# Channel mixing cut into six stages with a fixed turn on TensorE

## The chip, the cores and the metric

The kernel runs on one core of one Trainium2 chip. A core has five engines that each work through their own instructions in order and wait for one another by semaphores: TensorE (PE in the profile), VectorE (DVE), ScalarE (ACT), GpSimd (POOL) and SyncE (SP), which here issues every DMA. The metric is the time of one execution on the device in microseconds, the median over several executions.

## The reference

The input is x of 8 batches x 256 tokens x 512 channels, and a context of the same shape. Two blocks follow each other. The first is a transformer block: self-attention, cross-attention to the context, and an MLP of 512 to 2048 to 512, each with a layernorm ahead of it. The second is a recurrent block: time mixing (a scan over the tokens with a decaying state) and then channel mixing. The change lies in channel mixing, with the output of time mixing (`out`, `g`) and the residual `x`:

```python
og = normalised(out) * gn_w + gn_b
x1 = x + og * g @ Wo.T
xc = _ln(x1, ln2_w, ln2_b)
sx2 = jnp.concatenate([state[:, 0:1] - xc[:, :1], xc[:, :-1] - xc[:, 1:]], axis=1)
xk2 = xc + sx2 * ffn_maa_k
xr2 = xc + sx2 * ffn_maa_r
rr = jax.nn.sigmoid(xr2 @ Wfr.T)
kk = jnp.square(jax.nn.relu(xk2 @ Wfk.T))
return x1 + rr * (kk @ Wfv.T)
```

So there are four products of 256 x 512 by 512 x 512 for each batch: with Wo, Wfr, Wfk and Wfv.

## The kernel before

**Tiling.** A batch of 256 tokens is two tiles of 128 tokens (t = 0, 1), and the 512 channels are four chunks of 128 (KC). A product takes operands with the channels on partitions, so normalised rows are first transposed on TensorE (`to_t`, L217: eight 128 x 128 transposes for a batch, in two groups of four, one bank of PSUM each). Every operand of a product is split into a high and a low part in the fp32r type, and `mm3` (L185 to L187) adds three matmuls: high by high, high by low, low by high. `proj_n` gives tokens on partitions (24 matmuls of 512 columns for a batch, 12 for each token tile); `proj_t` gives channels on partitions (48 matmuls of 256 columns).

**Stages.** The whole program is straight code for 8 batches: self-attention, cross-attention, two halves of the MLP, then time mixing and channel mixing. Time mixing has stages a, b, e, c, d: a to e make its projections, c is the scan within blocks of 16 tokens and lies on GpSimd (L713 to L755) with sums on VectorE (L715, L730, L743, L762), d carries the state over the blocks: small transposes (L780, and L217 into the tile wtp), an update with 128 matmuls (L807), a scan on VectorE (L824), 128 output matmuls (L834), sums into on_ (L837) and a store of the normalised result to `yg` (L847). In the profile each L807 and L834 of the program shows as two matmuls.

d loads its first rows, dd, into a staging tile (L777). The two staging tiles (pool `wst`) go round between d's rows, the rows of v that ScalarE copies for c (L702, L703) and others; L703 writes into tiles that the c before it reads in L755.

**Channel mixing** has two stages for each batch, `front` (f) and `back` (g). f loads yg and g (L875, L877), transposes yg, scales and gates it (L883, L897), splits it (L890, L891), loads the residual x4 (L901, which the profile shows at the helper's line L288), multiplies by Wo and adds x4 (L902), normalises (`layernorm`, L194 to L205, with two small operations on GpSimd, L197 and L198), transposes again and makes xr and xk (`mixes`, L909 to L916, split by L890 and L891). g multiplies xr by Wfr and takes a tanh (L924), multiplies xk by Wfk and takes relu squared (L930, L931), split into kk (L932, L933), multiplies that by Wfv, gates, adds to x4 (L938, L939) and stores (L942).

**What sets the order.** `SEQ` lists the stages in the order in which they are written; each gets a priority from its batch and `AT` (L961: the smaller, the earlier), and a list scheduler, which goes by its own estimate of durations, then orders the instructions on each engine, so that stages of several batches interleave. Nothing else fixes the order of channel mixing's instructions on TensorE before the change. The order on an engine is fixed when the program is built, and on the chip no instruction passes another on its engine. Tiles share memory by the slots in `SLOTS` (x4 has two, a14 and a15) and PSUM by the banks in `BANKS`, each taken in turn.

Of the kernel before, what the change touches and what calls it, by code (L numbers as in the profile page):

```python
# [8 lines left out]
F32R = mybir.dt.float32r  # L9
# [8 lines left out]
P = 128  # L18
# [21 lines left out]
def slots(text):  # L40

    r = {}
    for item in text.split():
        name, at = item.split(":")
        r[name] = []
        for part in at.split(","):
            lo, _, hi = part.partition("-")
            r[name] += [f"{lo[0]}{i}" for i in range(int(lo[1:]), int((hi or lo)[1:]) + 1)]
    return r
# [20 lines left out]

SEQ = (
    "a0 b0 a1 e0 c0 b1 a2 e1 c1 d0 b2 a3 e2 c2 d1 b3 a4 e3 c3 d2 b4 a5 e4 c4 d3 b5 a6 e5 c5 d4 b6 a7 e6 c6 d5 b7 "
    "e7 c7 f0 d6 f1 g0 d7 f2 g1 f3 g2 f4 g3 f5 g4 f6 g5 f7 g6 g7"
)

BANKS = {
    "attn": slots("mm:k0,k1 sc:k2,k3 tr:k4,k5 cx:k6,k7"),
    "mlp": slots("tp:k4,k5 o:k0-k3 out:k6,k7"),
    "time": slots("tp:k2,k3 o:k0,k1 lo:k4 wtp:k5 up:k6,k7"),
    "chan": slots("tp:k2,k4 o:k0 o2:k1,k3"),  # L80
}

AT = {"a": -0.5, "b": -8.75, "e": 1.8, "c": -9.5, "d": -9.3, "f": 6.25, "g": 7.75}
PACE = 1000

def r32(ap):
    return ap.bitcast(F32)
# [3 lines left out]
def block_kernel(ctx: ExitStack, tc: tile.TileContext, a: dict, out: bass.AP):  # L93
# [29 lines left out]
    def c(name, i):  # L123
        at, _ = CV[name]
        return cv[:, at + i : at + i + 1]
# [3 lines left out]
    def wt(name, shape, dt=F32):  # L129
        tag = name  # L130
        if name in SLOTS[phase[0]]:
            tags = SLOTS[phase[0]][name]
            i = turn.get((phase[0], name), 0)
            turn[phase[0], name] = i + 1
            tag = tags[i % len(tags)]
        return wk.tile(shape, dt, name=name, tag=tag)
# [38 lines left out]
    def by_heads(name, i):  # L175
# [4 lines left out]
                nc.sync.dma_start(out=t[32 * hc : 32 * hc + 32, hm : hm + 1], in_=c(name, i + hc)[32 * hm : 32 * hm + 32, :])  # L180
        return t

    def mm3(o, ah, al, bh, bl, first, last):

        TE.matmul(o, ah, bh, start=first, stop=False)  # L185
        TE.matmul(o, ah, bl, start=False, stop=False)  # L186
        TE.matmul(o, al, bh, start=False, stop=last)  # L187

    def layernorm(x, xn=None, act=False):

        st = wt("st", [P, 2, 6])
        mv = wt("mv", [P, 2, 2])
        for t in range(2):
            V.bn_stats(st[:, t, :], x[:, t, :])  # L194
            V.bn_aggr(mv[:, t, :], st[:, t, :])  # L195
        rstd = wt("rstd", [P, 2])
        G.tensor_scalar(rstd, mv[:, :, 1], EPS, None, ALU.add)  # L197
        G.tensor_tensor(rstd, rstd, nhalf, ALU.pow)  # L198
        xn = x if xn is None else xn
        if act:  # L200
            nm = wt("nm", [P, 2])
            S.activation(nm, mv[:, :, 0], AF.Copy, scale=-1.0)
            for t in range(2):
                S.activation(nm[:, t : t + 1], nm[:, t : t + 1], AF.Copy, scale=rstd[:, t : t + 1])
                S.activation(xn[:, t, :], x[:, t, :], AF.Identity, bias=nm[:, t : t + 1], scale=rstd[:, t : t + 1])  # L205
            return xn
        for t in range(2):
            V.tensor_scalar(xn[:, t, :], x[:, t, :], mv[:, t, 0:1], rstd[:, t : t + 1], ALU.subtract, ALU.mult)
        return xn

    def to_t(xn, emit, kind="tp"):

        for k2 in range(2):
            tp = bank(kind, [P, 2, T])
            for kk in range(2):
                for t in range(2):
                    TE.transpose(tp[:, kk, t * P : (t + 1) * P], xn[t][:, (2 * k2 + kk) * P : (2 * k2 + kk + 1) * P], ident)  # L217
            emit(k2, tp)

    def both(x):  # L220
        return [x[:, t, :] for t in range(2)]
# [49 lines left out]
    def proj_n(ws, xts, emit, kind="o"):  # L271

        for t in range(2):
            ts = slice(t * P, (t + 1) * P)
            o = bank(kind, [P, D])
            n = len(ws)
            for u in range(n):
                (wh, wl), (xh, xl) = ws[u], xts[u]
                for k in range(KC):
                    mm3(o, xh[:, k, ts], xl[:, k, ts], wh[:, k, :], wl[:, k, :], u == 0 and k == 0, u == n - 1 and k == KC - 1)  # L280
            emit(t, o)
# [4 lines left out]
    def load_x(src, tag):  # L286
        x = wt(tag, [P, 2, D])
        nc.sync.dma_start(out=x, in_=tok(src))  # L288
        return x
# [572 lines left out]
        return v  # L862


    class ChannelMix:
        slots = "chan"

        def front(self, b, _):
            if b == 0:
                for n in ("o", "fr", "fk", "fv"):  # L870
                    W[n] = load_unit(a["w" + n])
                W["st0"] = wt("st0", [P, KC, NB])
                nc.sync.dma_start(out=W["st0"], in_=a["st0"])
            yn = wt("yn", [P, 2, D])
            nc.sync.dma_start(out=yn, in_=tok(yg[b]))  # L875
            g = wt("g", [P, KC, T])
            nc.sync.dma_start(out=g, in_=gt[b])  # L877

            def scaled(tp, k2, nm):

                for kk in range(2):
                    k = 2 * k2 + kk
                    S.activation(tp[:, kk, :], tp[:, kk, :], AF.Identity, bias=c(nm + "b", k), scale=c(nm + "w", k))  # L883
                return slice(2 * k2, 2 * k2 + 2)

            def parts():
                return wt("s", [P, KC, T], F32R), wt("s", [P, KC, T], F32R)

            def split_ps(hl_, ks, ps):
                S.copy(hl_[0][:, ks, :], ps)  # L890
                V.tensor_tensor(hl_[1][:, ks, :], ps, r32(hl_[0][:, ks, :]), ALU.subtract)  # L891

            yt = parts()

            def gated(k2, tp):
                ks = scaled(tp, k2, "gn")
                V.scalar_tensor_tensor(tp, tp, 0.5, g[:, ks, :], ALU.mult, ALU.mult)  # L897
                split_ps(yt, ks, tp)

            to_t(both(yn), gated)  # L900
            x4 = load_x(x3[b], "x4")  # L901
            proj_n([W["o"]], [yt], lambda t, o: V.tensor_tensor(x4[:, t, :], o, x4[:, t, :], ALU.add))  # L902
            xr, xk = parts(), parts()

            def mixes(k2, tp):
                ks = scaled(tp, k2, "n2")
                both_ = wt("xs", [P, 2, 2, T])
                xc, sx = both_[:, 0], both_[:, 1]
                S.copy(xc, tp)  # L909

                V.tensor_tensor(sx[:, :, 1:], tp[:, :, : T - 1], xc[:, :, 1:], ALU.subtract)
                V.tensor_tensor(sx[:, :, 0:1], W["st0"][:, ks, b : b + 1], tp[:, :, 0:1], ALU.subtract)
                for nm, y, hl_ in (("fmr", bank("o", [P, 2, T]), xr), ("fmk", tp, xk)):
                    for kk in range(2):
                        V.scalar_tensor_tensor(y[:, kk, :], sx[:, kk, :], c(nm, 2 * k2 + kk), tp[:, kk, :], ALU.mult, ALU.add)
                    split_ps(hl_, ks, y)  # L916

            to_t(both(layernorm(x4, wt("yn", [P, 2, D]), act=True)), mixes)
            return x4, xr, xk

        def back(self, b, got):
            x4, xr, xk = got
            rr = [wt("rr", [P, D]) for t in range(2)]
            proj_n([W["fr"]], [xr], lambda t, o: S.activation(rr[t], o, AF.Tanh, scale=0.5), "o2")  # L924
            kh = wt("kk", [P, KC, T], F32R)
            kl = wt("kk", [P, KC, T], F32R)

            def emit3(ks, o):
                kf = wt("kf", [P, 2, T])
                S.activation(kf, o, AF.Relu)  # L930
                V.scalar_tensor_tensor(o, o, 0.0, kf, ALU.max, ALU.mult)  # L931
                S.copy(kh[:, ks, :], o)  # L932
                V.tensor_tensor(kl[:, ks, :], o, r32(kh[:, ks, :]), ALU.subtract)  # L933

            proj_t(W["fk"], xk, emit3, "o2", pairs=True)

            def emit4(t, o):
                V.scalar_tensor_tensor(o, rr[t], 1.0, o, ALU.add, ALU.mult)  # L938
                V.scalar_tensor_tensor(x4[:, t, :], o, 0.5, x4[:, t, :], ALU.mult, ALU.add)  # L939

            proj_n([W["fv"]], [(kh, kl)], emit4, "o2")
            nc.sync.dma_start(out=tok(out[b]), in_=x4)  # L942


# [11 lines left out]
    def mix(n):  # L956
        for _ in range(min(n, len(seq))):
            stage, b = seq[0][0], int(seq.pop(0)[1:])
            if not base:
                base.append(tc.cur_priority)  # L960
            with tc.high_priority(tc.cur_priority - base[0] - int(PACE * (b + AT[stage]))):  # L961
                if stage in "fg":
                    run(cm, {"f": "front", "g": "back"}[stage], b, ("c", b))
                else:
                    run(tm, stage, b, ("t", b))

# [61 lines left out]
```

## Time and profile before

| | |
|---|---|
| median of three executions | 1972.2 us (1965.62 to 1973.21) |
| the profiled execution | 1968.74 us, span 1967.0 us |
| PE busy | 1731.9 us, 88% of the span |
| DVE busy | 1383.5 us, 70% |
| ACT busy | 1106.2 us, 56% |
| POOL busy | 744.7 us, 38% |
| mean granted clock of TensorE | 0.935 |
| last matmul of time mixing's last stage (L834) ends | 1807.45 us from the span's start |

Busy time is a share over stages with different limits. The page cuts the span into 40 slices of 49 us each; in its rows a digit is the busy share of an engine in tenths. A timeline row gives the start, the time from start to end, the engine, the line, the operation, the tile written and the tiles read, the shapes, and in brackets the engine's idle time before it and what ended that. Matmuls overlap: a row's time is longer than the distance to the next start. fr, fv and the output product show as `o<-whi,s` or `o<-whi,kk` with 128x512, fk as `o<-s,whi` with 128x256.

### The profile page before, as it was taken

What the parts mean: (1) busy time and instruction counts of PE and PEld (TensorE: products, weight loads), DVE (VectorE), ACT (ScalarE), POOL (GpSimd) and SP (SyncE); (2) the same over time, 40 slices, a digit from 0 to 9 for tenths busy, and PEclk for the clock granted to TensorE, in tenths of its full rate; (3) what the DMA queues carried; (4) which work ended last, traced back from release to release, by engine and by line L of the source; (5) the groups of instructions that cost most, each with busy time, mean ns of one, the idle gap of its engine ahead of it and who ended that gap; (6) DMA issues with size and microseconds to landing.
All of it is one profiled execution on the core that took longest, in us unless ns stands there. A gap on an engine that the chain in (4) does not pass through costs nothing.

```text
span 1967.0 us, 38765 instructions
## 1 busy us (share of the span) xinstructions
PE 1731.9 (88%) x14576; PEld 1449.5 (74%) x14576; DVE 1383.5 (70%) x3211; ACT 1106.2 (56%) x2745; POOL 744.7 (38%) x550
## 2 busy tenths in 40 slices
PE   4999999999899998999999998888888795789877
PEld 4777777777787776799999986676777573567766
DVE  4777767786778687665654354679778887988654
ACT  3877777877778688632332334354455354465342
POOL 2111111121222221232311100899999989992000
PEclk9999999999999999999999998998889786898989
DMA  6645444656555547322321133464656466443210
GB/s 188 160 125 123 119 118 119 185 154 164 133 143 137 148 129 208 114 89 75 108 65 65 54 118 105 113 161 126 168 128 166 130 186 194 131 121 98 75 64 22
DMA packets 237169, 247.35 MB, mean 126 GB/s; under 512 B 156291, under 2 KB 159243, under 8 KB 236982
## 3 DMA queue, kind: packets, MB, share of 16 engines
q1 hardware_dynamic: 236982, 244.87, 45.1%
q8 instruction: 115, 1.88, 0.4%
q14 instruction: 72, 0.59, 0.1%
HBM read 118.71 MB, written 58.98 MB: 90 GB/s over the span
## 4 chain that ended last, share of the span: by engine, by line
PE 58%; DVE 16%; POOL 7%; ACT 7%; DMA 6%; issue 4%; SPq 3%; DVEq 0%; POOLq 0%; ACTq 0%
PE o L185 7%; PE o L186 7%; PE o L187 7%; PE mm L185 5%; PE mm L186 4%; PE mm L187 4%; PE tr L366 3%; PE out L187 3%; PE out L186 3%; PE out L185 3%; DVE e L359 3%; PE cx L375 2%; POOL X L755 2%; DVE e L357 2%; PE sc L355 2%
## 5 line engine op out<-in xcount | busy, mean ns | idle before, releaser
L362 ACT ACTIVATE e<-e,mx 128x256 f32<-128x256 f32 x512 | 256.9, 506 | 44.3 <-DVE mx L359 43.1
L357 DVE TENSOR_TENSOR e<-sc,mc 128x512 f32<-128x512 f32 x256 | 172.4, 684 | 109.6 <-PE sc L355 56.1
L227 POOL TENSOR_TENSOR u<-y,u 128x1024 fp32r<-128x1024 f32 x32 | 78.6, 2456 | 440.9 <-ACT u L226 426.4
L359 DVE CUSTOM_DVE_ANT_0 e<-e,mn 128x256 f32<-128x256 f32 x512 | 223.3, 480 | 1.0
L755 POOL TENSOR_TENSOR X<-A,in 128x128 f32<-128x128 f32 (+14 forms) x120 | 208.3, 1772 | 12.0 <-DVE ob L762 9.7
L185 PE MATMUL o<-whi,s 128*128 128x512 f32 x320 | 148.1, 463 | 51.1 <-ACT s L890 32.1
L366 PE MATMUL tr<-ident,e 128*128 128x128 f32 x1024 | 172.1, 282 | 16.8 <-ACT e L362 14.0
L185 PE MATMUL mm<-u,whi 128*128 128x256 f32 x512 | 154.6, 303 | 12.0 <-DVE s L319 5.7
L370 ACT COPY pt<-tr 128x512 f32<-128x512 f32 x256 | 146.8, 581 | 28.7 <-PE tr L366 27.7
L366 PEld LDWEIGHTS tr<-ident,e 128*128 128x128 f32 x1024 | 120.6, 142 | 46.4 <-ACT e L362 23.6
L186 PE MATMUL mm<-u,whi 128*128 128x256 f32 x512 | 148.2, 289 | 4.2 <-POOL u L227 4.2
L187 PE MATMUL mm<-u,wlo 128*128 128x256 f32 x512 | 147.9, 289 | 0.0
L185 PE MATMUL o<-u,whi 128*128 128x256 f32 x512 | 144.5, 286 | 2.5 <-ACT hf L507 1.4
L187 PE MATMUL o<-u,wlo 128*128 128x256 f32 x512 | 144.0, 283 | 0.7 <-DVE wlo L172 0.6
L186 PE MATMUL o<-u,whi 128*128 128x256 f32 x512 | 143.9, 282 | 0.0
L186 PE MATMUL o<-wlo,s 128*128 128x512 f32 x320 | 140.9, 440 | 0.0
L355 PE MATMUL sc<-stk 128*128 128x256 f32 x512 | 116.9, 320 | 21.9 <-DVE e L357 16.4
L293 POOL TENSOR_TENSOR xr<-xr,row 128x512 f32<-128x512 f32 x48 | 65.6, 1387 | 186.0 <-DMA xr<-in_x 77.9
L187 PE MATMUL o<-whi,s 128*128 128x512 f32 x320 | 132.6, 432 | 0.0
L507 ACT ACTIVATE hf<-o,cv 128x256 f32<-128x256 f32 x128 | 59.6, 474 | 117.4 <-PE o L187 114.7
L197 POOL TENSOR_SCALAR rstd<-mv 128x2 f32<-128x2 f32 x48 | 15.5, 322 | 279.3 <-DVE mv L195 259.0
L185 PEld LDWEIGHTS o<-whi,s 128*128 128x128 f32 x320 | 69.3, 217 | 69.5 <-ACT s L890 33.6
(324 smaller groups left out, 5256.5 us busy)
## 6 DMA issues: line engine op xcount, KB each, us to landing
stk<-s SPq DMA_DIRECT2D x512, 128.0 KB, 2.4
x<-x SPq DMA_DIRECT2D x40, 512.0 KB, 4.7
x<-xr SPq DMA_DIRECT2D x24, 512.0 KB, 3.9
xr<-x SPq DMA_DIRECT2D x16, 512.0 KB, 4.7
w<-in_w SPq DMA_DIRECT2D x16, 512.0 KB, 6.3
w<-v SPq DMA_DIRECT2D x32, 256.0 KB, 3.1
x<-in_x SPq DMA_DIRECT2D x8, 512.0 KB
xr<-in_x SPq DMA_DIRECT2D x8, 512.0 KB, 3.6
```

Source lines behind the costliest of these rows:

```text
L185: TE.matmul(o, ah, bh, start=first, stop=False)
L186: TE.matmul(o, ah, bl, start=False, stop=False)
L187: TE.matmul(o, al, bh, start=False, stop=last)
L227: (eng or V).tensor_tensor(lo, y, r32(hi), ALU.subtract)
L293: G.tensor_tensor(x[:, t, :], x[:, t, :], r, ALU.add)
L355: TE.matmul(sc[:, t, :], qs[hm][:, hc, t * P : (t + 1) * P], ks[hm][:, hc, :], start=True, stop=True)
L357: V.tensor_tensor(e, sc, mc, ALU.mult)
L359: V.tensor_tensor_reduce(e[:, t, :], e[:, t, :], mn[:, t, :], 1.0, 3.0e38, ALU.add, ALU.min, accum_out=mx[:, kk2, hc, t : t + 1])
L362: S.activation(pr[:, t, :], e[:, t, :], AF.Exp, bias=mx[:, kk2, hc, t : t + 1], scale=-1.0, accum_out=sums[:, kk2, hc, t : t + 1])
L366: TE.transpose(pt_ps[:, kk, t * P : (t + 1) * P], pr[:, t, kk * P : (kk + 1) * P], ident)
L370: S.copy(pt, pt_ps)
L755: G.tensor_tensor(Y.rearrange("p (h j s) -> p h j s", h=4, j=16), A[:, t, 0:n, :].rearrange("p s h -> p h s").unsqueeze(2).broadcast_to([P ...
```

## The change

f and g are cut into six stages: p (loads of yg and g, transposes, gating), o (load of x4, output product, residual), t (layernorm, transposes, mixes), r (fr), k (fk) and v (fv, gate, residual, store). `SEQ` has a new order of them and `AT` a priority for each. The transposes of t and the products of o, r, k and v go through `in_turn`: its instructions on TensorE are ordered behind the last matmul of the unit that was written before it, so these units stand on TensorE in the order of `SEQ`. p and time mixing are not in the turn and may stand between or within the units. The output product uses the banks of "o2" (k1, k3); "o", now k0 and k5, is left to the mixes. The arithmetic is the same.

```diff
-    "e7 c7 f0 d6 f1 g0 d7 f2 g1 f3 g2 f4 g3 f5 g4 f6 g5 f7 g6 g7"
+    "e7 c7 p0 o0 d6 p1 t0 r0 o1 k0 p2 t1 v0 r1 d7 o2 k1 p3 t2 v1 r2 o3 k2 p4 t3 v2 r3 o4 k3 p5 t4 v3 r4 "
+    "o5 k4 p6 t5 v4 r5 o6 k5 p7 t6 v5 r6 o7 k6 t7 v6 r7 k7 v7"
...
-    "chan": slots("tp:k2,k4 o:k0 o2:k1,k3"),
+    "chan": slots("tp:k2,k4 o:k0,k5 o2:k1,k3"),
...
-AT = {"a": -0.5, "b": -8.75, "e": 1.8, "c": -9.5, "d": -9.3, "f": 6.25, "g": 7.75}
+AT = {
+    "a": -0.5, "b": -8.75, "e": 1.8, "c": -9.5, "d": -9.3,
+    "o": 6.25, "k": 7.4, "p": 5.55, "t": 6.65, "v": 7.9, "r": 7.1,
+}
...
-        TE.matmul(o, al, bh, start=False, stop=last)
+        latest[0] = TE.matmul(o, al, bh, start=False, stop=last)
...
+    def in_turn(unit):
+
+        with ExitStack() as turns:
+            if last[0] is not None:
+                turns.enter_context(tc.issue_after(last[0].ins))
+            unit()
+        last[0] = latest[0]
...
-            x4 = load_x(x3[b], "x4")
-            proj_n([W["o"]], [yt], lambda t, o: V.tensor_tensor(x4[:, t, :], o, x4[:, t, :], ALU.add))
-            xr, xk = parts(), parts()
+
+        def o(self, b):
+            self.x4[b] = x4 = load_x(x3[b], "x4")
+            in_turn(lambda: proj_n([W["o"]], [self.yt.pop(b)], lambda t, o: V.tensor_tensor(x4[:, t, :], o, x4[:, t, :], ALU.add), "o2"))
+
+        def t(self, b):
+            self.xr[b], self.xk[b] = xr, xk = parts(), parts()
...
-            to_t(both(layernorm(x4, wt("yn", [P, 2, D]), act=True)), mixes)
-            return x4, xr, xk
...
+            yn = layernorm(self.x4[b], wt("yn", [P, 2, D]), act=True)
+            in_turn(lambda: to_t(both(yn), mixes))
+
+        def r(self, b):
+            self.rr[b] = rr = [wt("rr", [P, D]) for t in range(2)]
+            in_turn(lambda: proj_n([W["fr"]], [self.xr.pop(b)], lambda t, o: S.activation(rr[t], o, AF.Tanh, scale=0.5), "o2"))
...
-            proj_t(W["fk"], xk, emit3, "o2", pairs=True)
+            in_turn(lambda: proj_t(W["fk"], self.xk.pop(b), emit3, "o2", pairs=True))
+
+        def v(self, b):
+            rr, x4 = self.rr.pop(b), self.x4.pop(b)
...
-            proj_n([W["fv"]], [(kh, kl)], emit4, "o2")
+            in_turn(lambda: proj_n([W["fv"]], [self.kk.pop(b)], emit4, "o2"))
```

The order on TensorE in the two built programs, from the last L780 of batch 5 on (a number is a batch, d5 to d7 are the L780, L807 and L834 of time mixing's d; the first transposes of yg and small pieces are left out; "/" joins units whose matmuls interleave):

```
before  d5 / r0 / k0 / o1   v0   t1   d6 / r1 / k1 / o2   v1 / t2 / d7 / r2 / k2 / o3 / v2   t3
        then for each batch b from 3 on:   r(b)   k(b) / o(b+1)   v(b) / o(b+1)   t(b+1)
change  t0   d5 / first half of r0   d6 / second half of r0   o1   k0   t1   v0 / r1 / d7   o2 / d7   k1 / d7
        then:   t2   v1   r2   o3   k2   t3   v2   r3   o4   k3   t4   v3   ...   t7   v6   r7   k7   v7
```

## The prediction

> **What bounds the kernel now.** The page comes first, its share table and its slices. TensorE (PE) is busiest over the whole span, but the slices tell three stories, and the change touches only the last quarter.
>
> ```profile
> span 1967.0 us, 38765 instructions
> ...
> PE   4999999999899998999999998888888795789877
> ...
> POOL 2111111121222221232311100899999989992000
> PEclk9999999999999999999999998998889786898989
> ```
>
> From slice 25 to 35 GpSimd (POOL) stands at 9: the scan part of time mixing (its stage c) paces the kernel, and TensorE has holes. From slice 36 on POOL is empty and what is left of channel mixing runs alone. The windows view over that part (columns: length; busy microseconds of PE, weight load, VectorE, ScalarE, POOL; granted clock; DMA share) gives the limit of each stretch:
>
> ```profile
> 1686.00:1719.00 33.00, 22.41 (x324) 18.91 (x322) 30.40 (x62) 10.27 (x20) 33.00 (x23) 0.86 0.45 151
> 1719.00:1752.00 33.00, 28.30 (x607) 23.24 (x607) 26.50 (x40) 18.13 (x43) 32.37 (x24) 0.87 0.39 100
> ...
> 1835.00:1868.00 33.00, 27.12 (x136) 22.45 (x136) 18.85 (x35) 13.85 (x28) 0.93 (x2) 0.90 0.21 65
> 1868.00:1901.00 33.00, 27.14 (x135) 22.81 (x136) 18.87 (x34) 13.35 (x27) 0.93 (x2) 0.84 0.19 64
> ```
>
> Up to 1752 POOL is full and VectorE nearly so. After 1808 no engine is full: a batch takes 33 us and PE is busy 27 of them at a clock of 0.84 to 0.90. The timeline of PE shows why; these are the rows where time mixing ends and where one batch of the tail turns into the next.
>
> ```profile
> 1804.21 3.24 PE L834 MATMUL up<-sts,r0t 32*32 32x64 f32 x128
> 1810.00 0.80 PE L185 MATMUL o<-whi,s 128*128 128x512 f32 x1 [2.55 <-ACT s L890]
> ...
> 1835.36 0.44 PE L217 MATMUL tp<-ident,yn 128*128 128x128 f32 x2 [0.50 <-ACT yn L205]
> 1836.07 0.87 PE L217 MATMUL tp<-ident,yn 128*128 128x128 f32 x6 [0.27 <-ACT yn L205]
> 1842.11 0.80 PE L185 MATMUL o<-whi,s 128*128 128x512 f32 x1 [5.17 <-ACT s L890]
> 1842.71 0.63 PE L186 MATMUL o<-wlo,s 128*128 128x512 f32 x1
> 1843.13 0.63 PE L185 MATMUL o<-whi,s 128*128 128x512 f32 x1
> ```
>
> PE transposes the normalised rows (L217), has nothing else in its queue, and waits 5.17 us until the first half of xr is mixed and split (L890). After that pause a 512-wide matmul starts every 0.427 us instead of every 0.233 us (18 of fv from 1957.9 on), about 12 times. The waits view of the tail names that one as PE's largest:
>
> ```profile
> PE o L185 <- ACT s L890: 23.2, 5, 5.2
> ```
>
> fr of batches 3, 4, 5, 6, 7 starts at 1810.00, 1842.11, 1875.17, 1908.72, 1940.93, so a round is 32.7 us on average; the last matmul starts at 1961.16 and the span ends 5.4 us after its end. The profiled execution took 1968.74 us, 1.7 over its span and 3.5 under the median of 1972.2. I work out a difference against the span and add it to the median.
>
> **The change, part by part.** It adds no arithmetic: matmuls, vector operations and DMAs are the same in number. It moves them.
>
> *A round in the new turn* is t(b+1), v(b), r(b+1), o(b+2), k(b+1). PE's work in it, at full clock: o, r, v have 24 matmuls of 512 each, 72 x 0.233 = 16.8 us; k has 48 of 256 at 0.120, 5.75; 16 transposes at 0.10, 1.6; in all 24.1 us. (By the same prices a round of before is 24.1 + 5.17 + 0.5 of pauses + 12 x 0.194 of slow clock = 32.1, near the 32.7 seen.)
>
> What each chain now hides behind: the layernorm chain from o's last matmul to the first transpose took 4.7 us (1863.73 to 1868.41) and gets k, 5.75 us; ScalarE has kf (L930, 0.60 us) ahead of it, so I leave 0.4 us open. The chain from the transposes to xr (5.17 us) gets v, 5.64 us. But VectorE and ScalarE are in order, and v's residual (L938 and L939, 0.62 us a start each) now falls among the mixes: of them, the first pair of L938 and L939 and the second pair's L911 and L915 stand ahead of the first split in the built order. That puts xr's high part at 2.8 + 1.2 + 0.3 + 3 x 0.41 + 0.6 + 0.6 = 6.7 us after the transposes and its low part at 8.3, while v ends at 6.2: pauses of 0.5 and 1.5. v itself waits 0.4 for kk's second pair (the row at 1956.84 has this wait, 0.42). Sum 2.9 us of pauses a round. Bounds: 0 (all hidden) and 5.67 (as before).
>
> The clock: pauses of 1.60, 0.79 and 0.41 between 1756.5 and 1760.7 left the matmuls that follow at 0.235, the 5.17 one did not. New pauses are of the first kind, so I take no slow matmuls; the other bound is 2.3 us a round. The Trainium skill, TensorE: Matmul & The Clock Gate, section "A second HAM failure mode: psum-queue depth-cycling", speaks against this: frequent short idles between groups of matmuls can set the clock back as well. By that rule the sum would be 14 us higher, by the rows it is not; I take the rows. So a round is 24.1 + 2.9 = 27.0 us, 5.7 less than before.
>
> *The turn against time mixing.* This part costs. In the order of before, 13 products stand on PE ahead of the last L834 of d7 (o, r, k, v of batches 0 to 2, and o of 3). In the order of the change there are 8: o, r, k, v of batch 0, o, r, k of batch 1, o of batch 2. Left behind it are v1, v2, r2, o3 (4 x 24 x 0.233 = 22.4), k2 (5.75) and three sets of eight transposes (2.4): 30.5 us of PE work moved into the tail. It is moved because a turn cannot be overtaken: r0's second half comes after d6's transposes and rows (L780, L807, L834), and everything of channel mixing comes after r0. d6's L780 waits for its load (L777), which waits for a staging buffer that ScalarE empties (L703) once POOL ends c6 at 1717.8:
>
> ```profile
> 1714.97 2.85 POOL X L755
> ...
> 1717.85 1.96 ACT in L703 x2
> ```
>
> Before, PE filled 1682 to 1718 with r0, k0, v0 and the second transposes; now it stands still there. When does d7's L834 end? Not before the data: by the in-order list, after d6 (24 us of its own chain from 1718, L777 to L834, as from 1718.95 to 1742.18 before) come r0's half, o1, k0, v0, r1, o2, k1 (2.8 + 4 x 5.6 + 2 x 5.75: 36.7 us), 2.5 of transposes and d7's own 8: about 47 us at full clock, ending at 1789 without any pause. At the pause share of 1653 to 1752 (25.4 of 99 us) it is 1806. Before it was 1807.45. I take no shift; bounds 1789 and 1815.
>
> *The sum*: from d7's end there are five rounds of (t, v, r, o, k) and a last t, v6, r7, k7, v7 of 23.4 + 3.6: 5 x 27.0 + 27.0 = 162 us, against 1961.56 - 1807.45 = 154.1 before. Difference +8 us.
>
> *Banks.* The output product moves from bank k0 to the o2 pair k1, k3; k0 and k5 serve the mixes. Before, o0's second half waited 5.02 us for L902 to empty k0, once, in POOL's stretch; zero in the tail, where that product was interleaved with fk. k5 is also time mixing's transpose bank, so d's transposes can wait for a mix (about 4.5 us, L915 to L891), at most at d6 and d7, and both lie within the bounds of d7's end. I take 0.
>
> *x4 and SP's queue.* x4 has two buffers. x4 of b+1 is loaded (L288) only after the store of b-1 (L942), which follows v(b-1). Before, the store was issued at 1801.40, the load at 1804.20, and its first reader (L902) ran at 1826.4: 18 us of slack. Now o(b+1) follows v(b-1) with only r between: L939 ends 4.6 us after v, the store takes 2.8 and the load about 4.4 (the page has 4.7, DMA being busier there), so the tile is there 12 us after v's end; o's first half is done at 2.1 + 5.6 + 0.4 + 2.8 = 11.0, and the layernorm chain starts to slip from 12.9 on. Cost 0 with 0.9 us to spare. The yn and g loads queued behind L942 and L288 on SP are for a batch further on and have over 10 us.
>
> **The rivals.**
> *The load of x4 takes the place of the wait for xr (slower).* If store and load take over 8.3 us together instead of 7.2 to 7.8, every further microsecond moves t and with it the round; at 2 us over, the pause also gets long enough for the slow clock: 5 x (1.2 + 2.3) = 17 us, 1997. For it: no slack. Against: DMA share in the tail is 0.08 to 0.21, so the load should be faster than the page's median.
> *The rounds do not shorten* because VectorE's order delays xr by more than I count: a round of 32 us, 6 x 5 = 30 us more, 2010. For it: VectorE works strictly in its order, and its 18.9 us of work a round would now fall in 27. Against: that is 70%.
> *Time mixing gains from the empty queues (faster).* With fewer vector operations of channel mixing in VectorE's way (30.40 of 33 us busy), d6 and d7 run earlier; at the bound of 1789 the result is 17 us lower, 1963. Against: POOL, not VectorE, paces c6 and c7.
> *All pauses vanish*: 6 x 2.9 = 17 us, 1963. Against: the in-order count above.
>
> **How the numbers follow.** 0.5% is 9.9 us, and the three runs of before lie 7.6 apart, so less than that can hardly be told from no change: 1962.3 to 1982.1 is "same". My own case, +8, has 0.50: 1980, own range 1970 to 1988, a fifth of it above 1982. The x4 load 0.22 (1997), longer rounds 0.10 (2010), earlier time mixing 0.11 and no pauses 0.07 (1963 each, not quite half below the bound). Slower: 0.10 + 0.22 + 0.10 = 0.42; faster: 0.08; same: 0.50. The range 1963 to 1999 leaves out 2010 and the lower ends.
>
> **What would show it.** Right: a hole on PE of about 35 us before d6's L780 near 1718; d7's last L834 within 1800 to 1815 with only k1 done; after it t, v, r, o, k in rounds of 26 to 28.5 us; no 5 us wait on L890; clock near 1.0 in the tail. Wrong: rounds over 30 us or under 25, a wait of L902 on the load of x4 of over 2 us, a clock under 0.9 in the tail, or d7 ending before 1795.

## The result, and the profile after

The changed kernel took 1979.99 us (median of 20 executions, 1972.08 to 1988.34) against 1971.91 us before (median of 20, 1965.07 to 1979.58): a ratio of 1.0043, 95% interval 1.0031 to 1.0056. Its profiled execution took 1973.26 us with a span of 1971.4, at the fast end of its own runs. From the page of the changed kernel (total; the 40 slices of PE and POOL; the granted clock of TensorE in tenths):

```profile
span 1971.4 us, 38802 instructions
...
PE   4999999999999997999999988888889894279998
...
POOL 2111111122212221232311100899999998990000
PEclk9999999999999999999999998898898876579999
```

PE falls to 4 and 2 in slices 33 and 34 (5 and 7 before; the first slice is 0) while POOL is at 8 and 9. From slice 36 on it stands at 9 but for one 8, where it had 9, 8, 7, 7. The windows view (length; busy time of PE, weight load, VectorE, ScalarE, POOL; granted clock; DMA share; GB/s) puts the two beside each other:

```profile
1686.00:1719.00 33.00, 2.47 (x83) 2.13 (x87) 18.00 (x34) 6.03 (x10) 33.00 (x22) 0.50 0.49 146
...
1830.00:1857.00 27.00, 25.07 (x135) 20.17 (x134) 17.40 (x34) 13.03 (x27) 0.93 (x2) 1.00 0.25 79
1857.00:1885.00 28.00, 25.99 (x141) 20.91 (x140) 18.05 (x35) 14.06 (x29) 0.93 (x2) 1.00 0.24 75
```

In the first stretch PE was busy 22.41 us before and is busy 2.47 now. In the tail it is busy 25 to 26 of 27 to 28 us, where it was 27 of 33, and the clock that stood at 0.84 to 0.90 is 1.00. The rows of PE's timeline behind this (the hole; the end of time mixing; then the waits of one round and its successor's first):

```profile
1712.87 0.60 PE L786 MATMUL wtp<-ident,w 16*128 16x16 f32 x4 [30.86 <-DMA w<-dd]
...
1799.76 1.93 PE L840 MATMUL up<-sts,r0t 32*32 32x64 f32 x128
...
1829.80 0.38 PE L223 MATMUL tp<-ident,yn 128*128 128x128 f32 x2
...
1833.07 0.50 PE L191 MATMUL o<-whi,kk 128*128 128x512 f32 x1 [0.33 <-ACT kk L959]
...
1839.82 0.50 PE L193 MATMUL o<-whi,s 128*128 128x512 f32 x1 [1.18 <-DVE s L893]
...
1857.92 0.33 PE L223 MATMUL tp<-ident,yn 128*128 128x128 f32 x1 [0.35 <-ACT yn L211]
```

(Lines moved down by 6 to 30: d's L780, L807, L834 are now L786, L813, L840; the mixes' L911 and L915 are L936 and L940; the split is L892 and L893; output residual L925, fv's residual L968 and L969, the store L972, the load of x4 L294.) d7's last L840 ends at 1801.69, 5.8 us earlier than before. From there to the end of the last matmul (1966.00) it is 164.3 us, 10.2 more than before. The rounds t, v, r, o, k start at 1801.85, 1829.80, 1857.19, 1884.69, 1912.15 and 1938.63: 27.4 us on average, against 32.7 before.

So the change did two large things that work against each other: every round is 5.3 us shorter, and eight products instead of 13 stand ahead of d7's end, so that four wide products and one fk more are left for the tail. Why they were pushed there is what the experiments are about; the waits view of 1680 us onward has the two largest steps of it:

```profile
PE wtp L786 <- DMA w<-dd: 30.9, 1, 30.9
ACT in L709 <- POOL X L761: 22.3, 1, 22.3
```

This is the chain that the prediction names: d6's first transposes wait for a load, the load for a staging buffer, the buffer for ScalarE's L709, that for POOL's scan. What is not said by it is why the rest of channel mixing stands behind those transposes.

### The profile page after: what moved, and what is told of

It is laid out like the page before. It is cut to its first block, busy times and chain, and to the rows that moved or that the text cites. A ratio compares the mean times of both kernels' runs of the same rounds, so it can differ in the third digit from the quotient of the medians.

```text
span 1971.4 us, 38802 instructions
## 1 busy us (share of the span) xinstructions
PE 1723.4 (87%) x14576; PEld 1440.2 (73%) x14576; DVE 1377.1 (70%) x3211; ACT 1103.5 (56%) x2745; POOL 742.2 (38%) x550
## 4 chain that ended last, share of the span: by engine, by line
PE 55%; DVE 16%; POOL 8%; ACT 7%; DMA 6%; issue 4%; SPq 3%; DVEq 0%; POOLq 0%; ACTq 0%
PE o L191 7%; PE o L193 7%; PE o L192 7%; PE mm L191 5%; PE mm L192 4%; PE mm L193 4%; POOL X L761 4%; PE out L193 3%; PE out L191 3%; PE out L192 3%; PE tr L372 3%; DVE e L365 3%; DVE e L363 2%; PE cx L381 2%; PE sc L361 2%
## 5 line engine op out<-in xcount | busy, mean ns | idle before, releaser
L191 PE MATMUL o<-whi,s 128*128 128x512 f32 x320 | 141.4, 442 | 19.3 <-ACT s L638 9.0
L193 PE MATMUL o<-whi,s 128*128 128x512 f32 x320 | 132.6, 425 | 7.2 <-DVE s L893 7.2
L192 PE MATMUL o<-wlo,s 128*128 128x512 f32 x320 | 135.7, 424 | 0.0
L743 POOL TENSOR_TENSOR X<-in 128x1024 f32<-128x1024 f32 x48 | 113.0, 2376 | 9.3 <-DVE A L749 9.2
```

Source lines behind the costliest of these rows:

```text
L193: latest[0] = TE.matmul(o, al, bh, start=False, stop=last)
L743: G.tensor_tensor(X.rearrange("p (i s d) -> p i s d", i=ni, s=m), rb[:, t0 : t0 + ni, :].unsqueeze(2).broadcast_to([P, ni, m, 64]), kb[:, ...
```

## The experiments

A ratio is to the kernel before, measured beside it on the same chip; in brackets is the 95% interval. Two theories for the hole: the prediction's (the turn: units cannot be overtaken, so everything waits for r0's second half) and its rival (the bank: k5 is the bank of d's tile wtp, and the second mix of each batch, now in k5 too, stands behind d for it).

**The mixes on k0 alone**, all else as in the change.

```diff
-    "chan": slots("tp:k2,k4 o:k0,k5 o2:k1,k3"),
+    "chan": slots("tp:k2,k4 o:k0 o2:k1,k3"),
```

> The changed kernel with one number taken out: the mixes use bank k0 alone, not k0 and k5 (k5 is also the bank of time mixing's small transposes, tile wtp); turn, stages and the output product's banks stay. Theory of the prediction (the turn holds r0's second half behind d6): the pause of about 31 us before d6's L780 stays, 8 products ahead of d7's last L834, about 1980 us. Rival (the shared bank k5 holds it: the mixes of xr's second half may take k5 only after d6's transposes): the pause is gone, 12 or more products stand ahead of d7's last L834, the rounds after it stay at 27.4 us, 1940 to 1952 us.

Measured: 1944.49 us, 0.988 [0.9863, 0.9898]. The hole is gone with the turn in place. In PE's timeline and the windows of this kernel d6's transposes have no wait ahead of them, and PE is busy 25.58 of the 33 us in which the change has 2.47:

```profile
1716.97 0.42 PE L786 MATMUL wtp<-ident,w 16*128 16x16 f32 x4
```

```profile
1686.00:1719.00 33.00, 25.58 (x248) 20.53 (x246) 31.18 (x67) 16.25 (x31) 32.87 (x22) 0.90 0.47 154
```

One bank more for the mixes costs 1.6% of the kernel (1.0043 to 0.988), some 32 us. The turn is not what made the hole.

**The kernel before with k5 added to its bank k0** (there the output product uses these banks as well).

```diff
-    "chan": slots("tp:k2,k4 o:k0 o2:k1,k3"),
+    "chan": slots("tp:k2,k4 o:k0,k5 o2:k1,k3"),
```

> The kernel before with one number added: bank o of channel mixing is k0 and k5 in place of k0; no six stages, no turn. Theory of the turn: no cost, 1965 to 1976 us. Rival of the shared bank: a pause of 20 us or more on PE before d6's L780, fewer products ahead of d7's last L834, rounds of 33 us as before, 1985 to 2005 us.

Measured: 1996.91 us, 1.0147 [1.0127, 1.0167]. The bank alone, without stages or turn, costs 29 us. The pause ahead of d6's L780 that the rival expected is not there; the products move all the same. d7 ends at 1793.36, 14.1 us earlier than before, and 17.4 wide products and 6 fk are left behind it instead of 14 and 5; the tail takes 197.1 us instead of 154.1. Inside time mixing fr waits twice for its operand (7.44 and 6.12 us; before, once, for 8.89). PE's timeline, and the waits from 1680 us on:

```profile
1697.55 0.79 PE L185 MATMUL o<-whi,s 128*128 128x512 f32 x1 [7.44 <-ACT s L890]
...
1755.62 0.80 PE L185 MATMUL o<-whi,s 128*128 128x512 f32 x1 [6.12 <-ACT s L890]
```

```profile
PE o L185 <- ACT s L890: 45.2, 8, 7.4
```

**The change without the turn**: the edges left out, stages and banks kept.

```diff
-            if last[0] is not None:
+            if False:
                 turns.enter_context(tc.issue_after(last[0].ins))
```

> The changed kernel without the edges that order the units (in_turn only calls the unit); stages, SEQ, AT and banks stay. Theory of the turn: r0 to v0 move up before d6, the pause goes, and the rounds lengthen towards 33 us as the units interleave again: 1950 to 1975 us. Rival of the shared bank: the pause of about 31 us stays; if the priorities alone keep the order, the rounds stay at 27 to 28 us too: 1978 to 1990 us.

Measured: 1989.02 us, 1.0112 [1.0086, 1.0138]. The hole is the same without the turn, as PE's timeline of this kernel shows:

```profile
1720.24 0.60 PE L786 MATMUL wtp<-ident,w 16*128 16x16 f32 x4 [30.90 <-DMA w<-dd]
```

This and the first experiment settle it from both sides. The turn by itself is a gain here (1.0112 to 1.0043, intervals apart). Where the gain lies is only in part shown: the tail is 3.4 us longer without the turn (167.7 against 164.3), and the rounds still come to 27.4 us from 1860 on. d7 ends later, at 1813.42, but it does so with the turn as well in two kernels below.

**The kernel before with its output product in o2.**

```diff
-            proj_n([W["o"]], [yt], lambda t, o: V.tensor_tensor(x4[:, t, :], o, x4[:, t, :], ALU.add))
+            proj_n([W["o"]], [yt], lambda t, o: V.tensor_tensor(x4[:, t, :], o, x4[:, t, :], ALU.add), "o2")
```

> The kernel before with the output product moved from bank k0 to k1 and k3 (o2), and nothing else. Both theories: the 5.02 us wait of o0's second half for L902 goes, in a stretch that GpSimd paces, so 1965 to 1977 us, no change that can be told.

Measured: 1983.97 us, 1.0076 [1.0051, 1.01]: both theories missed it. The profiled execution's span is 7.8 us over the one before (the medians lie 16 us apart), and its tail has one wait of nearly that size: x4's load was issued at 1828.7, after the store that frees its buffer (issued at 1822.6), and the residual L902, and with it PE, waited for it. Waits and PE's timeline of the tail of this kernel:

```profile
DVE x L902 <- DMA x<-x: 7.0, 1, 7.0
PE o L185 <- DVE x L902: 6.7, 1, 6.7
```

```profile
1833.84 0.80 PE L185 MATMUL o<-whi,s 128*128 128x512 f32 x1 [6.73 <-DVE x L902]
```

So the mechanism of the prediction's rival on x4 (a load behind a store) is real: in the order of before, with the product earlier, it cost PE 6.7 us once in the tail. That this wait is what the kernel loses is not shown. The rounds after it are shorter than before (31.0 to 32.5 us), and 15.0 wide products and 5.7 fk are left behind d7's end instead of 14 and 5.

**d6 written after t0.** This separates "two users of one bank get in each other's way" from "a bank goes to its users in the order in which the stages are written". Banks, priorities and turn stay; one unit changes its place in `SEQ`.

```diff
-    "e7 c7 p0 o0 d6 p1 t0 r0 o1 k0 p2 t1 v0 r1 d7 o2 k1 p3 t2 v1 r2 o3 k2 p4 t3 v2 r3 o4 k3 p5 t4 v3 r4 "
+    "e7 c7 p0 o0 p1 t0 d6 r0 o1 k0 p2 t1 v0 r1 d7 o2 k1 p3 t2 v1 r2 o3 k2 p4 t3 v2 r3 o4 k3 p5 t4 v3 r4 "
```

> The changed kernel with one unit moved in the written list: d6 stands after p1 and t0 instead of ahead of them. Banks (k0 and k5 for the mixes), priorities and the turn stay as in the change. Theory A (a bank goes to its users in the order in which the units are written: in the change t0's mixes stand behind d6's transposes for k5, d6 waits for POOL, and so r0 waits for POOL too): now t0's mixes have k5 before d6, r0, k0 and v0 fill the stretch, the 30.9 us hole ahead of d6's L786 falls below 8 us, and the time is 1945 to 1962 (not quite the 1944.5 of the mixes on k0 alone, since the mixes of t1 and d6 still share k5). Theory B (it is the sharing of k5 as such, in whatever order, with each side waiting for the other's evictions): the hole stays over 20 us or comes back as several waits at d6 and d7, 1972 to 1985. My prediction's reading (the turn cannot be overtaken) also says 1975 to 1985, for the turn is untouched.

Measured: 1962.46 us, 0.994 [0.9917, 0.9964], half a microsecond over the upper end of theory A and far under theory B. The rows to compare are VectorE's second pair of L940 for batch 0 (t0's second xr mix, the one in k5) and ScalarE's copy L822 that empties d6's wtp out of k5. In the change the first pair ran from 1659.58; the copies of d6 ran at 1726.89 and 1730.88, and the second pair came 2.1 us after the end of the last, behind two operations of time mixing on VectorE (L749, L830):

```profile
1730.88 0.58 ACT L822 COPY r0t<-wtp 128x512 f32<-128x512 f32 x1
```

```profile
1733.59 0.47 DVE L940 SCALAR_TENSOR_TENSOR o<-xs,cv,tp 128x256 f32<-128x256 f32 x1
1735.09 0.47 DVE L940 SCALAR_TENSOR_TENSOR o<-xs,cv,tp 128x256 f32<-128x256 f32 x1
```

With d6 written after t0 the pair runs 47 us earlier, and fr of batch 0 (from 1690.48), the output product of batch 1 (1701.55) and fk of batch 0 (1707.23) stand on PE where the hole was (VectorE's and PE's timelines of this kernel):

```profile
1686.69 0.47 DVE L940 SCALAR_TENSOR_TENSOR o<-xs,cv,tp 128x256 f32<-128x256 f32 x1
1689.33 0.48 DVE L940 SCALAR_TENSOR_TENSOR o<-xs,cv,tp 128x256 f32<-128x256 f32 x1
```

```profile
1690.48 0.80 PE L191 MATMUL o<-whi,s 128*128 128x512 f32 x1 [1.20 <-ACT s L892]
...
1701.55 0.50 PE L191 MATMUL o<-whi,s 128*128 128x512 f32 x1 [1.59 <-ACT rr L948]
...
1707.23 0.28 PE L191 MATMUL o<-s,whi 128*128 128x256 f32 x1
```

That is the cause of the hole. A bank is handed on in the order in which the stages are written; `SEQ` has d6 ahead of t0; d6 waits for POOL; so t0's second mix, r0 after it and all the rest wait for POOL as well, with the turn or without it. It is not all of the 32 us: the time stays 0.6% over that of k0 alone. That the later mixes, which still share k5 with d6 and d7, cost this rest is likely but not shown.

**The turn, where the bank does not bind**: mixes on k0 alone and no turn (the edits of the first and third experiment together).

```diff
-    "chan": slots("tp:k2,k4 o:k0,k5 o2:k1,k3"),
+    "chan": slots("tp:k2,k4 o:k0 o2:k1,k3"),
...
-            if last[0] is not None:
+            if False:
```

> The changed kernel with the mixes on bank k0 alone and without the turn's edges (the order is then by priorities). With the mixes on k0 alone and the turn, 1944.5 us were measured; the turn taken out with the banks of the change cost 9 us (1980.0 to 1989.0). Theory A (the turn earns its 9 us only where the shared bank makes the list bad; where PE can run ahead freely, a turn that cannot be overtaken costs a little): 1930 to 1943. Theory B (the turn's gain is in the rounds of the tail, by holding v between t and r, and is there whatever the banks): 1950 to 1958, with rounds over 28.5 us. With rounds of 27 to 27.5 us in the tail and 1944 to 1948 the turn does nothing.

Measured: 1937.65 us, 0.9826 [0.9796, 0.9855], the fastest of all. The rounds are as short without the turn: fk starts at 1818.24, 1845.35 and 1872.47. The windows of this kernel over one of them:

```profile
1845.00:1872.40 27.40, 25.76 (x139) 20.75 (x138) 17.66 (x34) 13.42 (x27) 0.93 (x2) 1.00 0.12 42
```

Theory A, that the turn costs a little where PE could run ahead, fits; against the first experiment (0.988 [0.9863, 0.9898]) the intervals lie apart, if barely, and the two were measured beside different executions of the kernel before, so the gain is not firm.

**fv's residual left out** (L969; the output then lacks fv's part, and x4's store does not wait for fv).

```diff
             def emit4(t, o):
                 V.scalar_tensor_tensor(o, rr[t], 1.0, o, ALU.add, ALU.mult)
-                V.scalar_tensor_tensor(x4[:, t, :], o, 0.5, x4[:, t, :], ALU.mult, ALU.add)
```

> The changed kernel without L969, the second of the two VectorE instructions that end fv (0.5 times the gated product is not added to x4, and x4 is stored as the output product left it; so x4's store also no longer waits for fv). The prediction's step: L968 and L969 fall among the mixes of t on VectorE and delay the split of xr; in the trace PE waits 1.18 us a round at L193 for L893. Theory A (that step is right): two instructions of 0.62 us less ahead of the split, the pause falls from 1.2 to 0.6 or less, a round from 27.4 to 26.2 to 26.9, the one wait for x4's load of 4.8 us goes as well, and the time is 1968 to 1976. Theory B (the mixes' own chain of scale, subtract, mix and split is what PE waits for, and VectorE does the residual in its idle time): the pause stays at 1.0 to 1.3 us, rounds 27.2 to 27.6; 1975 to 1981, the 4.8 us at most.

Measured: 1978.45 us, 1.0021 [0.9999, 1.0044]. The time does not tell it from the change (1.0031 to 1.0056). The trace does: the transposes of t start at 1843.21, 1869.92, 1896.70 and 1923.47, 26.7 to 26.8 us apart, and the pause of 1.18 us ahead of fr's low part has shrunk to 0.25 (PE's timeline of this kernel):

```profile
1879.81 0.50 PE L193 MATMUL o<-whi,s 128*128 128x512 f32 x1 [0.25 <-DVE s L893]
```

In the change VectorE's timeline shows what it was behind. Between the mixes of xr (L940 into o) and the split's low part (L893) stand two L968 and one L969:

```profile
1835.33 0.48 DVE L940 SCALAR_TENSOR_TENSOR o<-xs,cv,tp 128x256 f32<-128x256 f32 x1
1835.72 0.69 DVE L968 SCALAR_TENSOR_TENSOR o<-rr,o 128x512 f32<-128x512 f32 x1
1836.32 0.88 DVE L940 SCALAR_TENSOR_TENSOR o<-xs,cv,tp 128x256 f32<-128x256 f32 x2
1837.10 0.69 DVE L969 SCALAR_TENSOR_TENSOR x<-o,x 128x512 f32<-128x512 f32 x1
...
1838.48 0.69 DVE L968 SCALAR_TENSOR_TENSOR o<-rr,o 128x512 f32<-128x512 f32 x1
1839.08 0.69 DVE L893 TENSOR_TENSOR s<-o,s 128x512 fp32r<-128x512 f32 x1
```

In the profiled execution the six rounds' gain of about 4 us is met by a d7 that ends at 1812.56. What set that is open: among the profiled executions with d6 ahead of t0 in `SEQ` and the mixes on k0 and k5, d6's first transposes lie at 1712.87 (the change), 1720.24 (no turn), 1725.49 (here) and 1721.33 (the next).

**x4's load issued twice.**

```diff
             self.x4[b] = x4 = load_x(x3[b], "x4")
+            nc.sync.dma_start(out=x4, in_=tok(x3[b]))
```

> The changed kernel with the load of x4 (L294) issued twice into the same tile, so that the tile is complete 1 to 4.5 us later and everything else is the same. Theory A (the prediction's count: store, load, first reader with under 1 us to spare, so each further microsecond moves the transposes and with them the round): a wait of L925 on the load of 1 to 4 us in each round of the tail, rounds of 28.5 to 31 us, 1986 to 1998. Theory B (the chain has several microseconds of slack, the one wait of 4.8 us in the first round being an exception): no such waits in the later rounds, rounds of 27.4 us, 1978 to 1984.

Measured: 1996.21 us, 1.011 [1.0074, 1.0147]. The second load (L925 in this kernel) is issued when the first has landed, 3.5 us after it (SP's queue, and the waits of the tail):

```profile
1858.78 0.36 SPq L294 DMA_DIRECT2D x<-x  x1
1862.29 0.36 SPq L925 DMA_DIRECT2D x<-x  x1
```

```profile
DVE x L926 <- DMA x<-x: 20.3, 5, 8.6
```

The transposes of t start at 1813.77, 1843.50, 1872.98, 1901.99 and 1930.88: rounds of 28.9 to 29.7 us, 1.4 to 2.1 more than the change's in the same place. A delay of 3.5 us that costs 1.4 to 2.1 leaves 1.4 to 2.1 us of slack in the change: small, as theory A has it. The last round, up to t7 at 1961.26, takes 30.4 us, 3.9 more than in the change: no slack there. d7's end to the last matmul takes 177.3 us, 13.0 more than in the change, which is also what the ratios differ by (1.011 and 1.0043).

**The banks of before, with and without the turn.** Mixes and output product both on k0; stages as in the change.

```diff
-    "chan": slots("tp:k2,k4 o:k0,k5 o2:k1,k3"),
+    "chan": slots("tp:k2,k4 o:k0 o2:k1,k3"),
...
-            in_turn(lambda: proj_n([W["o"]], [self.yt.pop(b)], lambda t, o: V.tensor_tensor(x4[:, t, :], o, x4[:, t, :], ALU.add), "o2"))
+            in_turn(lambda: proj_n([W["o"]], [self.yt.pop(b)], lambda t, o: V.tensor_tensor(x4[:, t, :], o, x4[:, t, :], ALU.add)))
```

> The six stages and the turn with the banks exactly as in the kernel before: mixes and output product both on k0, o2 pair for the rest. Theory A (the only bank that matters is k5; the output product's place is worth little while the turn spaces its users): 1938 to 1950, like the 1944.5 of the mixes on k0 with the product in o2. Theory B (product and mixes on one bank wait for each other's evictions: in the turn t, v, r, o the bank goes from the last mix to the product with only v and r between): 1952 to 1966, with a pause of 1 to 3 us a round at the output product or at the transposes.

> The six stages with the banks of the kernel before and without the turn's edges, so the split into stages with their own priorities alone. With the mixes on k0 and the product in o2 the turn taken out gave 1937.65 us. Theory A (the turn costs a little wherever PE could run ahead): 1930 to 1948 here too. Theory B (the turn is what keeps the users of one bank apart: without it the output product of the batch ahead and the mixes hold k0 against each other, and PE waits in line behind them): 1955 to 1975, with waits of PE of several microseconds on evictions L925 or splits L892/L893.

Measured: with the turn 1946.39 us, 0.9872 [0.983, 0.9913]; without it 1972.73 us, 1.0 [0.9976, 1.0025]. With the turn the output product's place is worth nothing (0.988 with o2). Without turn and o2 the six stages fall back into the pattern of before: fv ahead of the transposes, nothing to do after them, and the long wait for xr (PE's timeline, waits from 1680 us on, and the windows of one round):

```profile
1842.00 0.79 PE L191 MATMUL o<-whi,s 128*128 128x512 f32 x1 [5.18 <-ACT s L892]
...
1842.60 0.63 PE L192 MATMUL o<-wlo,s 128*128 128x512 f32 x1
1843.02 0.63 PE L191 MATMUL o<-whi,s 128*128 128x512 f32 x1
```

```profile
PE o L191 <- ACT s L892: 19.5, 6, 5.2
```

```profile
1842.00:1875.60 33.60, 26.84 (x136) 22.44 (x136) 18.37 (x35) 13.72 (x27) 0.93 (x2) 0.91 0.19 62
```

Here each matmul after the wait starts 0.42 or 0.43 us after the last one instead of 0.23, and the round is back at 33.6 us. So the short rounds come from the order t, v, r, and either the turn or the product in o2 is enough to get it. Why the product's bank does so is not shown.

**Closer batches in the priorities** on top of the fastest kernel.

```diff
-PACE = 1000
+PACE = 700
```

> The fastest so far (mixes on k0 alone, no turn: 1937.65 us) with the constant PACE at 700 instead of 1000, which closes up the batches in the priorities and changes the order from early on. Theory A (the order still puts work into PE's stretches of waiting, and closer batches put a little more ahead of d7's end): 1928 to 1936. Theory B (the tail's rounds of 27 us and time mixing's pace on POOL are what is left, and neither hangs on PACE): 1936 to 1942. If closing up delays time mixing's stages: over 1945.

Measured: 1945.26 us, 0.9875 [0.9834, 0.9917]: no gain. The median lies 7.6 us over the same kernel with 1000, with overlapping intervals, at the edge of what had been put to a delay of time mixing. The profiles agree with that as far as they go: the tail is as long as there (125.4 us), and d7 ends 3.8 us later (1809.93 against 1806.17).

The variants of the six stages side by side, with the work that is left behind d7's last L840, counted in PE's timeline (o, r and v as 24 matmuls of 512 columns each, k as 48 of 256):

| mixes | output product | turn | ratio | o, r, v left | k left | tail, us |
|---|---|---|---|---|---|---|
| kernel before: k0 | k0 | none | 1 | 14.0 | 5.0 | 154.1 |
| k0, k5 (the change) | o2 | yes | 1.0043 | 18.0 | 6.0 | 164.3 |
| k0, k5 | o2 | no | 1.0112 | 18.0 | 6.2 | 167.7 |
| k0, k5, d6 after t0 | o2 | yes | 0.994 | 15.0 | 6.0 | 144.1 |
| k0 | o2 | yes | 0.988 | 13.5 | 5.0 | 125.7 |
| k0 | o2 | no | 0.9826 | 14.0 | 5.0 | 125.3 |
| k0 | k0 | yes | 0.9872 | 13.5 | 5.0 | 127.6 |
| k0 | k0 | no | 1.0 | 14.0 | 5.0 | 149.4 |

The last columns give the balance of the change. With the work left as before (14 and 5; mixes on k0, product in o2, no turn) the short rounds take the tail from 154.1 to 125.3 us, 28.8 less. Four wide products and one fk more, with their transposes and pauses, take it from 125.3 to 164.3, 39.0 more. The rest, up to the 4.4 us by which the profiled spans differ, is d7's earlier end.

## Why the prediction was right, and where it was not

**The number: right.** +8 us was forecast, and the medians differ by 8.1. The sum's two sides hold as well: 162 us of tail against 164.3 measured. In the profiled pair the difference is only 4.4 us, since d7 ended 5.8 us earlier than before where the sum took no shift (1801.69, inside its bounds of 1789 and 1815). That profile is the second fastest of the change's 20 executions, 6.7 us under their median, and in the three variants with the same banks and written order (no turn, no residual, load twice) d7 ends at 1811.35 to 1813.42. So how the 8.1 us of the medians divide between the tail and d7's end is not known, and that they match the sum so closely may in part be luck.

**The turn against time mixing: the size right, the cause wrong.** Eight products ahead of d7's end instead of 13, a hole of about 35 us before d6's L780 (30.86 measured), v1, v2, r2, o3, k2 moved into the tail: all of it is there. But the step says "It is moved because a turn cannot be overtaken". That is the step that was wrong. With the turn and the mixes on k0 alone there is no hole; without the turn and with k5 there is the same hole. r0's second half did stand behind d6's rows in the built order; what put it there was the bank.

**Banks: "I take 0" was wrong by some 32 us** (the change against the mixes on k0 alone). The step looked at k5 from one side only: d's transposes might wait for a mix, for 4.5 us at most. The other side decided, a mix waiting for d's transposes, and these wait for POOL. It went unseen in the sum because its whole effect had been read off the built order and booked under the turn. The total survived by that; the advice that a reader would draw from it, to loosen the turn, would have made the kernel slower (1.0112). The Trainium skill, Perfetto Trace Analysis, section "Matmul Optimizations", asks that all eight banks be used. Here one bank more for the mixes, a bank that time mixing uses too, cost 1.6%; the measurement decides.

**The round: 27.0 forecast, 27.4 measured.** The pauses lie where they were put: kk 0.33 (0.4 forecast), xr's low part 1.18 (1.5), the layernorm chain 0.28 to 0.35 (0.4); xr's high part costs about 0.15 instead of 0.5. That fv's residual delays xr's split is shown by the kernel without it (pause 0.25, round 26.8). The idle column sums to 0.9 us less than forecast and the round is still 0.4 longer. The mis-sized term is what a pause costs: from fv's first start (1831.10) to fr's first (1837.94) it is 6.84 us, where 24 x 0.233 is 5.6, though the idle column shows 0.33 and about 0.15. In the timeline a matmul lasts 0.39 us and the next starts 0.233 after it; a pause loses this overlap of 0.16 as well, the matmul after a pause has its successor only 0.34 later, and the column leaves both out. Two slips in the step are small beside this: its four pauses (0.4, 0.5, 1.5, 0.4) add to 2.8, not 2.9, and by its own 6.7 and 8.3, less two matmuls, the low part's pause is 1.1, near the 1.18 measured.

**The clock: right.** With the 5.17 us wait gone, the granted clock is 1.00 in every round, pauses of up to 1.3 us notwithstanding. The rule weighed against it (the Trainium skill, TensorE: Matmul & The Clock Gate, "A second HAM failure mode: psum-queue depth-cycling") does not show in this kernel's tail; the six stages with waits of 4.7 to 5.2 us (mixes and product on k0, no turn) stand at 0.88 to 0.91 there.

**x4: nearly right.** The step took 0 with 0.9 us to spare; the doubled load shows 1.4 to 2.1 in all rounds but the last. Two waits for the load are left (waits of the changed kernel's tail, fr's low part beside them, and the two rows in VectorE's timeline):

```profile
PE o L193 <- DVE s L893: 7.2, 6, 1.3
DVE x L925 <- DMA x<-x: 5.5, 2, 4.8
```

```profile
1821.75 0.69 DVE L925 TENSOR_TENSOR x<-o,x 128x512 f32<-128x512 f32 x1 [0.70 <-DMA x<-x]
...
1930.66 0.69 DVE L925 TENSOR_TENSOR x<-o,x 128x512 f32<-128x512 f32 x1 [4.83 <-DMA x<-x]
```

The wait of 4.83 us stands in the last round, not in the first, where the expectation for the doubled load has it. For most of it VectorE had nothing else to do: the first half of o7, which L925 needs as well, ended only at 1930.31. In the first round the product's half ended at 1821.40. So the load cost some 0.35 us in each of the two.

**The rivals.** The late load came in the first and last round, not in every one, and cost little. Among the six-stage kernels long rounds (33.6 us) came only without the turn and with the product on k0. Time mixing's gain from empty queues, if it is one, is the 5.8 us of d7's end; by the spread of d6's start among the kernels with the same written order and banks (1712.87 to 1725.49) it may as well be the run. The rival that mattered was missing: that the change's own bank, and not its order, sets the loss.

## What to carry to other kernels

When a stage gets a bank or buffer that a later-written stage also uses, look for both directions of the wait, and take the written order, not the priorities, as the order in which it is handed on: the slowest user in that order sets the time of the next. When a built order shows work moved, do not stop at the newest constraint that could explain it; take each constraint out alone. Where two large terms nearly cancel (here 29 us won and 39 us lost in the tail), a right total says little of either; test the terms.

## What was not expected of the hardware

A pause costs TensorE more than the idle column shows: 24 matmuls with pauses of 0.33 and 0.15 us in the column took 1.24 us more than 24 x 0.233. After a wait of 5.18 us the matmuls started every 0.43 us for about 5 us, while pauses of 1.18 us every round left a start every 0.233 us and a granted clock of 1.00. And the output product's bank is worth 1.7% without the turn (1.0 to 0.9826) and nothing with it (0.9872 to 0.988).
